# Two-layer recurrent and mixture-of-experts block on one core: recurrence pieces moved into the listing of rows, two weight loads moved among stores, row normalization moved to ScalarE

## The chip, the core and the metric

The program runs on one core of a Trainium2 chip. A core has a matrix engine (TensorE, PE in the profile; its weight loads are listed as PEld), three elementwise engines (VectorE as DVE, ScalarE as ACT, GpSimd as POOL) and a queue engine (SyncE as SP) that mostly issues DMAs. Every engine runs its own list of instructions in order and waits on semaphores where an operand isn't there yet; so an instruction that waits holds up all that is listed behind it on that engine. The metric is the time in microseconds of one execution of the whole program, as a median of runs.

## The reference

The input is one sequence of 2048 rows of 512 numbers. There are two layers; each computes `x + s * silu(f)`, where `s` is a mixer and `f` a mixture-of-experts network, both fed with the layer-normalized `x`. The change is in layer 0, cut here to what matters:

```python
xn = layernorm(x)
# mixer: token shift, three projections, a recurrence over time for each of 512 channels
xk, xv, xr = xn*tm + shifted(xn)*(1 - tm)          # three different tm
k, v, r = xk @ Wk.T, xv @ Wv.T, sigmoid(xr @ Wr.T)
for t in range(2048):                              # aa, bb, pp carried
    qt = max(pp, k[t] + u);  e1 = exp(pp - qt);  e2 = exp(k[t] + u - qt)
    wkv[t] = (e1*aa + e2*v[t]) / (e1*bb + e2)
    pn = max(pp - exp(w), k[t]);  f1 = exp(pp - pn);  f2 = exp(k[t] - pn)
    aa, bb, pp = f1*aa + f2*v[t], f1*bb + f2, pn
s = (r * layernorm(wkv, ln_g, ln_b)) @ Wo.T
# experts: each row goes to one of 2 by the larger gate logit
sel = argmax(xn @ gate_w.T)
f = top_w * ((silu(xn @ w_gate[sel].T) * (xn @ w_up[sel].T)) @ w_down[sel].T)
```

Layer 1 is an attention with pooled keys and a network of 16 routed and 2 shared experts; the change leaves its code alone.

## The kernel before

**First stage (L170 to L362).** Eight loads bring `x` to SBUF as `xin` (two tiles of 128 rows each, L177), and one brings Wk (L182). For each pair of tiles VectorE makes mean and variance (L129, L130), ScalarE normalizes in place (L234), and VectorE takes the difference of the two gate logits of each row (L238, into `dl`). Then each tile is turned by four PE transposes (L139), copied to `xt` by ScalarE (L140; three buffers) and stored by SP to a DRAM tensor `xnt0`, which holds the normalized rows turned (L245; 16 stores). Wv and Wr are loaded behind these stores (L248, L249). From `dl` VectorE then makes the listing: two small matmuls count the rows of each expert (L271), a chain of small VectorE operations (L277 to L337) gives every row a place in a list sorted by expert, VectorE makes one-hot tables (`put` L343, `hot` L350), and 16 matmuls (L355, 32 PE instructions[...]) turn these into the list `tok` of row numbers with `row_mr`, each listed row's mean and reciprocal deviation (L359, L360).

**Recurrence (L386 to L536).** `recurrence(b)` handles 256 time steps for all channels, eight blocks in all. It is a generator of 22 pieces, so that its work can be laid among other work piece by piece. In order: load the turned rows `xT` and take the difference `diff` to the row before (piece 1, POOL, L400); mix for k (2); mix for v and project half of k (3); mix for r and project the other half of k (4); two pieces with scans on k and the projections of v (5, 6); two with the projections of r and the differences under the exponentials (7, 8, L459 to L465); two sigmoids (9, L467, L468); two exponentials (10, L470, L471); scans `st_a` and `st_b` (L478), divisions, a normalization and the store. The carried states are columns 0 of `st_p`, `st_a`, `st_b`; block b starts with three ScalarE copies of the last column (L397). The projections share two PSUM buffers (`proj`), each free again when ScalarE has copied it out (L428, L430, L452, L467, L468).

**Layer 0's experts (L540 to L650).** The list is worked off in pairs of tiles. `rows0` gathers 128 rows per tile with an indirect DMA from POOL (`xr`, L545), normalizes them on VectorE with `row_mr` (L552), turns them with four PE transposes through one PSUM buffer (L560) and copies them to `xg` on ScalarE (L563). `up0` makes 16 PE instructions per unit (L571), a Silu on ScalarE (L576, `sg`) and a product on VectorE (L578, `hT`); `down0` (L593) runs two units later. Weights come in eight parts per pair through four buffers (`load0`, L157 and L161).

**What sets the order.** The program text gives each instruction a priority, and a scheduler at build time puts them in an order for each engine: what is ready earlier by its own estimate of times goes first, and among ready ones the text decides. Work can so be listed far ahead of its place in the text. `tc.keep_in_program_order(ins)` forbids this for one instruction: it stays behind all that the text has before it on its engine. Seven pieces of the recurrence stand in the text ahead of the experts (L692); from there on `pieces0` and the recurrence alternate, paced by `done * WORK < spent * PIECES * NRB` (L697).

Of the kernel before, what the change touches and what calls it, by code (L numbers as in the profile page):

```python
# [9 lines left out]
F32 = mybir.dt.float32  # L10
I32 = mybir.dt.int32
AF = mybir.ActivationFunctionType
ALU = mybir.AluOpType
# [4 lines left out]
P = 128  # L18
# [59 lines left out]
def tile_kernel(ctx: ExitStack, tc: tile.TileContext, a: dict):  # L78
# [89 lines left out]


# [55 lines left out]
    for i in range(0, NT, 2):  # L225
        xin = xins[i // 2]
        mv, rstd = norm_stats(xin, 2, all_mv[:, i : i + 2, :], facts[:, 2, i : i + 2])
        shift = small.tile([P, 2], F32, tag="shift", name="shift")
# [3 lines left out]
        for j in range(2):  # L232
            xn = xin[:, j, :]
            nc.scalar.activation(  # L234
                xn, xn, AF.Identity, bias=shift[:, j : j + 1], scale=rstd[:, j : j + 1],
            )
            junk = n0.tile([P, D], F32, tag="hot", bufs=2, name="junk")
            nc.vector.tensor_tensor_reduce(  # L238
                out=junk, in0=xn, in1=wdiff, scale=1.0, scalar=0.0, op0=ALU.mult, op1=ALU.add,
                accum_out=dl[:, i + j : i + j + 1],  # L240
            )
    for i in range(NT):
        xt = n0.tile([P, NC, P], F32, tag="xt", name="xt")
        transposed(n0ps, xins[i // 2][:, i % 2, :], xt, "tp")
        nc.sync.dma_start(out=xnt0[:, :, i * P : (i + 1) * P], in_=xt)  # L245
    wv = rc.tile([P, NC, D], F32, name="wv")
    wr = rc.tile([P, NC, D], F32, name="wr")
    tc.keep_in_program_order(nc.sync.dma_start(out=wv, in_=a["Wv"]))  # L248
    tc.keep_in_program_order(nc.sync.dma_start(out=wr, in_=a["Wr"]))  # L249
    nc.vector.tensor_copy(facts[:, 1, :], all_mv[:, :, 0])  # L250

    sel = n0.tile([P, NT, E0], F32, bufs=1, name="sel")
    nc.vector.tensor_scalar(
        out=sel[:, :, 0], in0=dl, scalar1=0.0, scalar2=None, op0=ALU.is_le
    )
    nc.vector.tensor_scalar(
# [83 lines left out]

    put = n0.tile([P, NT, 3, NST], F32, bufs=1, name="put")
# [6 lines left out]
    for i0 in range(0, NT, HN):  # L348
        hot = n0.tile([P, HN, P], F32, tag="hot", bufs=2, name="hot")
# [20 lines left out]
    zero = rc.tile([P, DX], F32, name="zero")  # L370
    nc.gpsimd.memset(zero, 0.0)
    S4 = [P, NC, RB]
    ones = rc.tile([P, P], F32, name="ones")
    nc.vector.memset(ones, 1.0 / D)
    nge = rc.tile([P, NC], F32, name="nge")
    nc.scalar.activation(nge, vecs[:, VEC.index("decay"), :], AF.Exp)
    nc.vector.tensor_scalar(out=nge, in0=nge, scalar1=-1.0, scalar2=None, op0=ALU.mult)

    st_p = rc.tile([P, NC, RB + 1], F32, name="st_p")
    st_a = rc.tile([P, NC, RB + 1], F32, name="st_a")  # L380
    st_b = rc.tile([P, NC, RB + 1], F32, name="st_b")
    nc.vector.memset(st_p[:, :, 0:1], -1.0e38)
    nc.vector.memset(st_a[:, :, 0:1], 0.0)
    nc.vector.memset(st_b[:, :, 0:1], 0.0)

    def recurrence(b):  # L386

        t0 = b * RB

        xT0 = rb.tile([P, NC, RB + 1], F32, tag="xT0", bufs=2, name="xT0")  # L390
        if b == 0:
            nc.vector.memset(xT0[:, :, 0:1], 0.0)
            nc.sync.dma_start(out=xT0[:, :, 1:], in_=xnt0[:, :, 0:RB])
        else:
            nc.sync.dma_start(out=xT0, in_=xnt0[:, :, t0 - 1 : t0 + RB])
            for st in (st_p, st_a, st_b):
                nc.scalar.copy(st[:, :, 0:1], st[:, :, RB : RB + 1])  # L397
        cur, prev = xT0[:, :, 1 : 1 + RB], xT0[:, :, 0:RB]
        diff = rb.tile(S4, F32, tag="diff", name="diff")
        nc.gpsimd.tensor_tensor(out=diff, in0=cur, in1=prev, op=ALU.subtract)  # L400
        yield

        def mixed(tm):
            xm = rb.tile(S4, F32, tag="xm", bufs=3, name="xm")
            for c in range(NC):
                nc.vector.scalar_tensor_tensor(
                    out=xm[:, c, :], in0=diff[:, c, :], scalar=vec(tm, c),
                    in1=prev[:, c, :], op0=ALU.mult, op1=ALU.add,
                )
            return xm  # L410

        def project(xm, w_, o0):
            ps = rps.tile([P, 2, RB], F32, tag="proj", name="proj")
            for j in range(2):
                for c in range(NC):
                    nc.tensor.matmul(  # L416
                        out=ps[:, j, :], lhsT=w_[:, c, (o0 + j) * P : (o0 + j + 1) * P],
                        rhs=xm[:, c, :], start=(c == 0), stop=(c == NC - 1),
                    )
            return ps  # L420

        k = rb.tile(S4, F32, tag="k", name="k")
        ku = rb.tile(S4, F32, tag="ku", name="ku")
        v = rb.tile(S4, F32, tag="v", name="v")
        r = rb.tile(S4, F32, tag="r", name="r")

        def take_k(o0, ps):
            nc.scalar.copy(k[:, o0 : o0 + 2, :], ps)  # L428
            for j in range(2):
                nc.scalar.activation(  # L430
                    ku[:, o0 + j, :], ps[:, j, :], AF.Identity, bias=vec("first", o0 + j)
                )

        def scan_p(c):
            nc.vector.tensor_tensor_scan(
                out=st_p[:, c, 1 : RB + 1],
                data0=nge[:, c : c + 1].to_broadcast([P, RB]),
                data1=k[:, c, :], initial=st_p[:, c, 0:1], op0=ALU.add, op1=ALU.max,
            )

        xk = mixed("tm_k")
        yield
        xv = mixed("tm_v")
        take_k(0, project(xk, wk, 0))
        yield
        xr = mixed("tm_r")
        take_k(2, project(xk, wk, 2))
        yield
        for o0 in (0, 2):
            scan_p(o0)  # L450
            scan_p(o0 + 1)
            nc.scalar.copy(v[:, o0 : o0 + 2, :], project(xv, wv, o0))  # L452
            yield
        pp, ppn = st_p[:, :, 0:RB], st_p[:, :, 1 : RB + 1]
        ex = rb.tile([P, 4, NC, RB], F32, tag="ex", name="ex")
        e1, e2, f1, f2 = (ex[:, i] for i in range(4))
        qt = rb.tile(S4, F32, tag="qt", name="qt")
        r01 = project(xr, wr, 0)
        nc.vector.tensor_tensor(out=f1, in0=pp, in1=ppn, op=ALU.subtract)  # L459
        nc.vector.tensor_tensor(out=f2, in0=k, in1=ppn, op=ALU.subtract)  # L460
        yield
        r23 = project(xr, wr, 2)
        nc.vector.tensor_tensor(out=qt, in0=pp, in1=ku, op=ALU.max)  # L463
        nc.gpsimd.tensor_tensor(out=e1, in0=pp, in1=qt, op=ALU.subtract)  # L464
        nc.gpsimd.tensor_tensor(out=e2, in0=ku, in1=qt, op=ALU.subtract)  # L465
        yield
        nc.scalar.activation(r[:, 0:2, :], r01, AF.Sigmoid)  # L467
        nc.scalar.activation(r[:, 2:4, :], r23, AF.Sigmoid)  # L468
        yield
        nc.scalar.activation(ex[:, 2:4], ex[:, 2:4], AF.Exp)  # L470
        nc.scalar.activation(ex[:, 0:2], ex[:, 0:2], AF.Exp)  # L471
        fv = qt
        nc.vector.tensor_tensor(out=fv, in0=f2, in1=v, op=ALU.mult)
        yield

        def scan(st, add, cs):
            for c in cs:
                nc.vector.tensor_tensor_scan(  # L478
                    out=st[:, c, 1 : RB + 1], data0=f1[:, c, :], data1=add[:, c, :],
                    initial=st[:, c, 0:1], op0=ALU.mult, op1=ALU.add,  # L480
                )

        scan(st_a, fv, (0, 1))
        nc.gpsimd.tensor_tensor(out=v, in0=e2, in1=v, op=ALU.mult)
        yield
        scan(st_a, fv, (2, 3))
        yield
        scan(st_b, f2, range(NC))
        yield
        num, den = ku, fv  # L490
        nc.vector.tensor_tensor(out=num, in0=e1, in1=st_a[:, :, 0:RB], op=ALU.mult)
        nc.gpsimd.tensor_tensor(out=den, in0=e1, in1=st_b[:, :, 0:RB], op=ALU.mult)
        yield
        nc.vector.tensor_tensor(out=num, in0=num, in1=v, op=ALU.add)
        nc.vector.tensor_tensor(out=den, in0=den, in1=e2, op=ALU.add)
        yield
        for c0 in (0, 2):
            for c in (c0, c0 + 1):
                nc.vector.reciprocal(out=den[:, c, :], in_=den[:, c, :])
            yield  # L500


        two = rb.tile([P, 2, RB], F32, tag="two", name="two")

        def mean(src):

            nc.vector.tensor_tensor(out=two, in0=src[:, 0:2], in1=src[:, 2:4], op=ALU.add)
            nc.vector.tensor_tensor(
                out=two[:, 0, :], in0=two[:, 0, :], in1=two[:, 1, :], op=ALU.add
            )  # L510
            pm = f0t.tile([P, 2, RB], F32, tag="tp", name="pm")[:, 0, :]
# [1374 lines left out]
```

## Time and profile before

| what | value |
|---|---|
| median of 3 runs | 1950.14 us (1944.71 to 1953.96) |
| the profiled execution | 1940.83 us |
| its span, first to last instruction | 1939.1 us |
| PE busy | 1857.2 us (96%) |
| PEld, DVE, ACT, POOL busy | 1292.1, 787.3, 532.9, 465.9 us |
| mean granted TensorE clock | 0.986 of full speed |
| DMA bytes, mean rate | 381.35 MB, 197 GB/s |
| first matmul of the experts (L571) | at 82.32 us |

Times within the span count from its first instruction. In a line of the timeline the columns are start, duration, engine, source line, operation, output and inputs, shape and count; brackets at the end give the engine's idle time before it and the instruction that ended it. In a table of stretches each engine has its busy time and count, then follow the granted TensorE clock (PEclk, 1.00 is full speed), the DMA engines' mean busy share and the rate in GB/s.

### The profile page before, as it was taken

How to read it: one execution, taken by the hardware profiler on the slowest of the kernel's cores; microseconds unless marked ns; L12 is line 12 of the kernel's file. 1: busy time of each engine (PE TensorE's matmuls, PEld its weight loads, DVE VectorE, ACT ScalarE, POOL GpSimd, SP SyncE). 2: the span in 40 equal slices, each digit the busy share in tenths (PEclk: the TensorE clock that was granted, in tenths of full speed). 3: DMA queues.
4: the chain of work that ended last, by engine and by line, in shares of the span. 5: the costliest groups of instructions: out<-in, count | busy, mean ns of one | idle time of the engine just before them, and what ended most of it. 6: DMA issues, size and time to landing. Idle time of an engine off the chain costs nothing.

```text
span 1939.1 us, 23212 instructions
## 1 busy us (share of the span) xinstructions
PE 1857.2 (96%) x8107; PEld 1292.1 (67%) x8107; DVE 787.3 (41%) x1565; ACT 532.9 (27%) x994; POOL 465.9 (24%) x350
## 2 busy tenths in 40 slices
PE   5899999999999999999989999999999999999977
PEld 4677777787877777777533654444767777777654
DVE  8713627272634545252166544331323232223116
ACT  6212322232323232232134212221222222222223
POOL 1301212121201111020210453000344444444430
PEclk9799999999999999999999999999999999999998
DMA  7548685635654443436461553022999999999963
GB/s 250 205 144 278 205 306 178 221 108 163 197 195 141 130 131 125 157 98 233 147 227 46 174 215 114 31 95 87 313 290 316 320 311 298 292 282 265 299 148 131
DMA packets 214096, 381.35 MB, mean 197 GB/s; under 512 B 16972, under 2 KB 134476, under 8 KB 213080
## 3 DMA queue, kind: packets, MB, share of 16 engines
q1 hardware_dynamic: 183896, 332.78, 50.7%
q0 software_dynamic: 28784, 45.63, 10.7%
q10 hardware_dynamic: 1296, 1.41, 0.3%
q8 instruction: 67, 1.10, 0.2%
q14 instruction: 53, 0.43, 0.1%
HBM read 294.04 MB, written 85.72 MB: 196 GB/s over the span
## 4 chain that ended last, share of the span: by engine, by line
PE 83%; DMA 6%; DVE 3%; issue 2%; POOL 2%; ACT 2%; SPq 0%; POOLq 0%; ACTq 0%; DVEq 0%
PE pg L571 23%; PE py L593 12%; PE ph L1685 9%; PE py L1709 9%; PE proj L416 7%; PE py L1105 4%; PE ph L956 3%; PE pw L1593 2%; DMA comb<-y,to 2%; PE pq L1352 2%; PE tp L1678 1%; PE po L712 1%; PE ps L1560 1%; PE pl L870 1%; PE pw L1477 1%
## 5 line engine op out<-in xcount | busy, mean ns | idle before, releaser
L571 PE MATMUL pg<-xg,w 128*128 128x256 f32 (+1 forms) x2304 | 497.8, 369 | 3.3 <-ACT xg L563 3.3
L571 PEld LDWEIGHTS pg<-xg,w 128*128 128x128 f32 x2304 | 420.9, 191 | 95.0 <-issue 42.1
L1717 POOL DMA_INDIRECT comb<-y,to x146 | 226.9, 1554 | 300.0 <-DMA comb<-y,to 222.2
L593 PE MATMUL py<-wd,hT 128*128 128x512 f32 x544 | 256.9, 593 | 2.9 <-DVE hT L578 2.9
L1685 PEld LDWEIGHTS ph<-xg,w 128*128 128x128 f32 (+1 forms) x1776 | 201.9, 182 | 39.8 <-ACT xg L1680 32.9
L1685 PE MATMUL ph<-xg,w 128*128 128x128 f32 (+1 forms) x1776 | 214.4, 277 | 1.5 <-DMA w<-in_w_dram 1.5
L1709 PE MATMUL py<-w,ht 128*128 128x512 f32 (+1 forms) x438 | 209.1, 593 | 0.0
L578 DVE TENSOR_TENSOR hT<-sg,pg 128x256 f32<-128x256 f32 (+1 forms) x144 | 57.0, 402 | 338.4 <-ACT sg L576 338.3
L576 ACT ACTIVATE sg<-pg 128x256 f32<-128x256 f32 (+1 forms) x144 | 53.5, 372 | 419.7 <-PE pg L571 419.4
L593 PEld LDWEIGHTS py<-wd,hT 128*128 128x128 f32 x544 | 102.1, 190 | 72.2 <-issue 61.9
L1714 DVE TENSOR_SCALAR y<-py,g 128x512 f32<-128x512 f32 x73 | 54.6, 749 | 206.7 <-PE py L1709 196.1
L942 ACT ACTIVATE ht<-ph,b1t 128x128 f32<-128x128 f32 (+1 forms) x222 | 81.3, 366 | 178.9 <-PE ph L1685 161.4
L1709 PEld LDWEIGHTS py<-w,ht 128*128 128x128 f32 (+1 forms) x438 | 75.1, 191 | 49.8 <-issue 49.3
L1680 ACT COPY xg<-tp 128x512 f32<-128x512 f32 x74 | 43.4, 586 | 177.2 <-PE tp L1678 166.4
L1105 PE MATMUL py<-w,hT 128*128 128x512 f32 (+1 forms) x192 | 89.3, 596 | 0.0
L956 PE MATMUL ph<-xT,w 128*128 128x512 f32 (+1 forms) x192 | 88.0, 597 | 0.0
L1043 POOL DMA_INDIRECT xs<-acc,slot x64 | 63.1, 985 | 67.2 <-DMA xs<-acc,slot 43.5
L1352 PE MATMUL pq<-xT,wqg 128*128 128x256 f32 x224 | 56.6, 401 | 14.2 <-DVE wide L1572 9.6
L712 PE MATMUL po<-wo,yb 128*128 128x512 f32 x128 | 59.3, 620 | 9.6 <-ACT acc L721 5.5
L416 PE MATMUL proj<-xm,wr 128*128 128x256 f32 x256 | 60.9, 393 | 5.6 <-ACT v L452 5.6
L464 POOL TENSOR_TENSOR ex<-st_p,qt 128x1024 f32<-128x1024 f32 x8 | 18.3, 2288 | 193.0 <-DVE qt L463 193.0
L1678 PEld LDWEIGHTS tp<-ident,x 128*128 128x128 f32 x296 | 36.7, 140 | 38.8 <-issue 21.5
(418 smaller groups left out, 2180.9 us busy)
## 6 DMA issues: line engine op xcount, KB each, us to landing
w<-in_w_dram SPq DMA_DIRECT2D x76, 704.0 KB
w<-in_w_dram SPq DMA_DIRECT2D x76, 512.0 KB
w<-in_w_gate_dram SPq DMA_DIRECT2D x72, 512.0 KB
w<-in_w_up_dram SPq DMA_DIRECT2D x72, 512.0 KB
wd<-in_w_down_dram SPq DMA_DIRECT2D x72, 512.0 KB
xs<-zero SPq DMA_DIRECT2D x16, 1360.0 KB
x<-xs SPq DMA_DIRECT2D x74, 272.0 KB
w<-in_w_dram SPq DMA_DIRECT2D x76, 192.0 KB
```

What stands on the lines that cost most here:

```text
L416: nc.tensor.matmul(out=ps[:, j, :], lhsT=w_[:, c, (o0 + j) * P : (o0 + j + 1) * P], rhs=xm[:, c, :], start=(c == 0), stop=(c == NC - 1),)
L571: nc.tensor.matmul(out=pg[:, i, 0:n], lhsT=w[:, c, i * FH + f * P : i * FH + (f + 1) * P], rhs=xg[:, c, 0:n], start=(c == 0), stop=(c == N ...
L593: nc.tensor.matmul(out=p, lhsT=hT[:, u * P : (u + 1) * P], rhs=wd[:, f, :], start=first_, stop=last_,)
L712: nc.tensor.matmul(out=po, lhsT=yb[:, c, s * P : (s + 1) * P], rhs=wo[:, c, :], start=(c == 0), stop=(c == NC - 1),)
L942: nc.scalar.activation(dst, src, AF.Relu, bias=b)
L956: nc.tensor.matmul(out=ph[0:n, :], lhsT=up(w, f, n, c), rhs=xT[:, c, cols], start=(c == 0), stop=(c == NC - 1),)
L1043: ins = nc.gpsimd.indirect_dma_start(out=xs, out_offset=bass.IndirectOffsetOnAxis(ap=slot[:, i, k : k + 1], axis=0), in_=acc[:, i, :], in_ ...
L1105: nc.tensor.matmul(out=py, lhsT=hT[0:n, e, f, s * P : (s + 1) * P], rhs=down(w, f, n), start=(e == 0 and f == 0), stop=(e == NS - 1 and f ...
L1352: nc.tensor.matmul(out=pq[:, j, :], lhsT=w[:, c, w0 : w0 + P], rhs=xT[:, c, tc0], start=(c == 0), stop=(c == NC - 1),)
L1685: nc.tensor.matmul(out=ph[0:n, :], lhsT=up(w, f, n, c), rhs=xg[:, c, :], start=(c == 0), stop=(c == NC - 1),)
L1709: nc.tensor.matmul(out=py, lhsT=hT[0:n, f, :], rhs=down(w, f, n), start=(f == 0), stop=(f == NF1 - 1),)
L1717: nc.gpsimd.indirect_dma_start(out=c_, out_offset=bass.IndirectOffsetOnAxis(ap=to, axis=0), in_=y[:, h * D // 2 : (h + 1) * D // 2], in_of ...
```

## The change

1. The whole text from the constants `zero`, `ones`, `nge` and the states to the end of `recurrence` moves from behind the listing to the head of the first stage. This lets pieces be drawn earlier: two ahead of `sel`, one ahead of `put`, one between the second and third `hot` table. So `done` starts at 4, and two more pieces stand ahead of the experts: six in all instead of seven.
2. Pins: the first instruction of the listing (`sel`) stays behind the two pieces on VectorE; block 0's two exponentials stay behind all earlier ScalarE text, its sigmoids included; block 1's three state copies stay behind all earlier ScalarE text, that of the experts included.
3. `diff` of blocks 0 and 1 is made on VectorE instead of POOL.
4. Wv is loaded behind the fifth store of a turned tile, Wr behind the ninth, instead of both behind the sixteenth.
5. Gathered rows are normalized on ScalarE as scale times row plus bias. The bias is minus mean times reciprocal deviation, which was made anyway for L234; it now goes straight into the table `facts`, and the copy of the means (L250) falls away.

```diff
@@ ahead of the first stage: zero .. recurrence, moved here; changed lines of it alone @@
             for st in (st_p, st_a, st_b):
-                nc.scalar.copy(st[:, :, 0:1], st[:, :, RB : RB + 1])
+                ins = nc.scalar.copy(st[:, :, 0:1], st[:, :, RB : RB + 1])
+                if b == 1:
+                    tc.keep_in_program_order(ins)
...
-        nc.gpsimd.tensor_tensor(out=diff, in0=cur, in1=prev, op=ALU.subtract)
+        (nc.vector if b < 2 else nc.gpsimd).tensor_tensor(
+            out=diff, in0=cur, in1=prev, op=ALU.subtract
+        )
...
-        nc.scalar.activation(ex[:, 2:4], ex[:, 2:4], AF.Exp)
-        nc.scalar.activation(ex[:, 0:2], ex[:, 0:2], AF.Exp)
+        ins = nc.scalar.activation(ex[:, 2:4], ex[:, 2:4], AF.Exp)
+        if b == 0:
+            tc.keep_in_program_order(ins)
+        ins = nc.scalar.activation(ex[:, 0:2], ex[:, 0:2], AF.Exp)
+        if b == 0:
+            tc.keep_in_program_order(ins)
@@ first stage @@
-        shift = small.tile([P, 2], F32, tag="shift", name="shift")
+        shift = facts[:, 1, i : i + 2]
...
+    wv = rc.tile([P, NC, D], F32, name="wv")
+    wr = rc.tile([P, NC, D], F32, name="wr")
     for i in range(NT):
...
         nc.sync.dma_start(out=xnt0[:, :, i * P : (i + 1) * P], in_=xt)
-    wv = rc.tile([P, NC, D], F32, name="wv")
-    wr = rc.tile([P, NC, D], F32, name="wr")
-    tc.keep_in_program_order(nc.sync.dma_start(out=wv, in_=a["Wv"]))
-    tc.keep_in_program_order(nc.sync.dma_start(out=wr, in_=a["Wr"]))
-    nc.vector.tensor_copy(facts[:, 1, :], all_mv[:, :, 0])
-
+        for at, w_, nm in ((4, wv, "Wv"), (8, wr, "Wr")):
+            if i == at:
+                tc.keep_in_program_order(nc.sync.dma_start(out=w_, in_=a[nm]))
+
+    blocks = (piece for b in range(NRB) for piece in recurrence(b))
+    for _ in range(2):
+        next(blocks)
     sel = n0.tile([P, NT, E0], F32, bufs=1, name="sel")
-    nc.vector.tensor_scalar(
+    ins = nc.vector.tensor_scalar(
         out=sel[:, :, 0], in0=dl, scalar1=0.0, scalar2=None, op0=ALU.is_le
     )
+    tc.keep_in_program_order(ins)
...
+    next(blocks)
     put = n0.tile([P, NT, 3, NST], F32, bufs=1, name="put")
...
     for i0 in range(0, NT, HN):
+        if i0 == 2 * HN:
+            next(blocks)
         hot = n0.tile([P, HN, P], F32, tag="hot", bufs=2, name="hot")
@@ rows0 @@
-            nc.vector.tensor_scalar(
-                out=xr, in0=xr, scalar1=row_mr[:, 0, j : j + 1],
-                scalar2=row_mr[:, 1, j : j + 1], op0=ALU.subtract, op1=ALU.mult,
+            nc.scalar.activation(
+                xr, xr, AF.Identity, bias=row_mr[:, 0, j : j + 1], scale=row_mr[:, 1, j : j + 1]
             )
@@ the main loop @@
-    blocks = (piece for b in range(NRB) for piece in recurrence(b))
-    done = 0
+    done = 4
...
-    for _ in range(7):
+    for _ in range(6 - done):
```

## The prediction

> **What bounds the kernel now.** I read the page's engine shares first: PE is busy for 1857.2 of 1939.1 us, so only PE's idle time (82 us) and its time at a lower clock can be won. The table of stretches says where these lie: from 100 to 480 us PE is never idle, the rest of the idle time is mostly the change of layers at 940 to 1100 us and the end from 1850 us, which the change leaves alone. The first 100 us are what it touches:
>
> ```profile
> 30.00:40.00 10.00, 10.00 (x53) 8.39 (x52) 8.11 (x26) 6.53 (x12) 1.97 (x1) 1.00 0.70 207
> 40.00:50.00 10.00, 4.58 (x25) 4.08 (x23) 8.28 (x30) 3.07 (x7) 0.37 (x1) 0.85 0.94 306
> 50.00:60.00 10.00, 10.00 (x41) 9.06 (x41) 5.72 (x9) 1.91 (x1) 3.80 (x3) 0.63 1.02 373
> 60.00:70.00 10.00, 4.45 (x18) 3.50 (x17) 7.26 (x8) 4.17 (x5) 5.65 (x4) 0.88 1.07 371
> 70.00:80.00 10.00, 8.99 (x36) 7.22 (x34) 9.53 (x13) 1.46 (x4) 4.44 (x2) 0.78 0.12 44
> ```
>
> Columns: PE, PEld, DVE, ACT, POOL busy, then clock, DMA share, GB/s. PE loses 5.42 us in 40 to 50 and 5.55 us in 60 to 70, the clock is below full from 46 us to about 90, and the DMA engines are saturated from 40 to 70. The timeline names the gaps (last bracket of a line):
>
> ```profile
> 47.36 7.07 PE L355 MATMUL tab<-put,hot 128*128 128x51 f32 x32 [5.42 <-DVE put L343]
> 54.23 8.67 PE L416 MATMUL proj<-xm,wv 128*128 128x256 f32 x32
> 68.45 6.64 PE L416 MATMUL proj<-xm,wr 128*128 128x256 f32 x16 [5.55 <-ACT v L452]
> 82.32 13.44 PE L571 MATMUL pg<-xg,w 128*128 128x256 f32 x48 [3.33 <-ACT xg L563]
> 97.31 3.62 PE L571 MATMUL pg<-xg,w 128*128 128x256 f32 x16
> ```
>
> The second and third gap both end with ScalarE, so I read its own list, and VectorE's row normalizations beside it:
>
> ```profile
> 57.04 1.91 ACT L470 ACTIVATE ex<-ex 128x2048 f32<-128x2048 f32 x1 [12.56 <-DVE ex L460]
> 63.72 0.20 ACT L397 COPY st_p<-st_p 128x4 f32<-128x4 f32 x1 [4.76 <-POOL ex L464]
> 66.01 1.91 ACT L471 ACTIVATE ex<-ex 128x2048 f32<-128x2048 f32 x1 [2.09 <-POOL ex L465]
> 67.83 1.05 ACT L452 COPY v<-proj 128x512 f32<-128x512 f32 x2
> 79.56 0.20 ACT L397 COPY st_a<-st_a 128x4 f32<-128x4 f32 x1 [3.36 <-DVE ku L491]
> 81.59 0.20 ACT L397 COPY st_b<-st_b 128x4 f32<-128x4 f32 x1 [1.83 <-POOL qt L492]
> 81.69 0.58 ACT L563 COPY xg<-tp 128x512 f32<-128x512 f32 x1
> 62.74 4.44 DVE L552 TENSOR_SCALAR xr<-xr,row_mr 128x512 f32<-128x512 f32 x3 [4.59 <-issue]
> ```
>
> The `v` copies need only PE's projection, done at 62.9, but are listed behind block 1's `st_p` copy and block 0's second exponential, which wait for POOL's L464 and L465, and these sit behind four gathers. PE waits for a `proj` buffer meanwhile. The last `xg` copy (transposes done at about 78.2) stands behind the `st_a` and `st_b` copies in the same way. So the gaps are an order of listing on ScalarE, not a lack of work.
>
> **The pins.** Block 1's copies and block 0's exponentials are just the four instructions in front of those two. Behind the pins they can't stand there: the exponentials come after the sigmoids, the copies after the first Silus. What that returns: the gap of 5.55, the gap of 3.33, and clock. The `wr` run above took 6.64 us for 16 against 3.62 for 16 at 97 us, so 3.0 lost; the experts' first 48 took 13.44 against three times 3.45 (16 instructions' pitch in the chain of waits), so 3.1 lost. Here a rule weighs in: the Trainium skill, TensorE: Matmul & The Clock Gate, section "What's actually happening", lets PE fall to half clock after an idle window of some 3.4 us and recover after about 3.4 us of work; by it each gap costs half of 3.4, 1.7 us, and the two returns would be 3.4 in place of 6.1. The trace has clock 0.50 for about 6 us after each of these gaps, so I take 6.1. Price of the pins: VectorE's scans L478 wait for later exponentials, and behind them in its list stand the experts' products L578. Estimate 0 to 5 us, once; I take 0, since `down0` runs two units (two times 5.17 us) behind.
>
> **PE's new sequence.** The listing's matmuls end at 54.43 now. Then `wv` 8.67, still cold; `wr` 32 instructions at full pitch 6.9; two sets of transposes at 0.60; then the experts, at 54.4 + 8.7 + 6.9 + 1.2 = 71.2 if nothing is late. Gathered rows must be there: the first landed at 62.74 (VectorE stood ready from 58.2), and then come two normalizations at 0.80, two transposes at 0.60, two copies at 0.58, some 4 us: 66.7. That lies ahead of 71.2, so PE's own work decides. If `wr` is left behind the start, the start is 66.7 and 6.9 us of work come later: equal to 73.6. Drawing six pieces instead of seven therefore costs at most 2.4 us; I take 0.
>
> **Wv and Wr.** Each is 1024 KB; at 373 GB/s (row of 50 to 60) both take 5.6 us. Now they are issued at 44.35 and 45.02, and expert weights queue behind. After, they go at about 24 and 31, ahead of 11 and 7 stores. Gain: the saturated stretch that the gathers run in ends up to 5.6 us earlier; I count 0, since PE decides. With Wv there, `wv` projections could also fill PE's gap of 5.42 us, which would give up to that and its 1.8 us of cold loss (8.67 against 6.9); whether they are listed there nothing in this trace tells. From 0 to 7.2; I take 0. Loss: SP's issue of 0.62 and 0.44 is small, but the stores queue in the DMA engines behind 1 MB each. A store already takes 3.5 us and more (the load of `xT` waits 2.0 us for one), and there are three `xt` buffers, so ScalarE's copy of tile i+3 waits for the store of tile i: the trace has the copy at 27.03 some 0.1 us behind the landing of the fourth store. A delayed copy holds ScalarE, behind it the normalizations L234, then L238 and `sel`. From 0 to 5.6; I take 2, as two normalizations already stand between such copies.
>
> **`diff` and the copy of the means.** POOL's `diff` takes 1.89 us (L400); VectorE has 1.22 for the same shape (L459), so twice 1.22 are added to VectorE. Taken away are the copy L250 (1.81 us) and the stretching of L288:
>
> ```profile
> 26.34 1.81 DVE L250 COPY facts<-all_mv 128x16 f32<-128x16 f32 x1
> 38.03 2.33 POOL L400 TENSOR_TENSOR diff<-xT 128x1024 f32<-128x1024 f32 x1 [9.92 <-DVE run L279]
> 38.59 1.79 DVE L288 TENSOR_TENSOR full<-run,eno 128x8 f32<-128x8 f32 x1
> ```
>
> L288 handles 8 elements; its neighbours of that size take 0.15, so 1.64 us of it is the POOL instruction beside it. Net 1.81 + 1.64 - 2.44 = 1.0 us earlier on the path from `dl` to `tok`, all on VectorE, which is busy there. With the 2 us of the stores the listing is 1 us later: start 72.2.
>
> **Rows on ScalarE.** 0.80 us (L234, same shape, scale and bias from SBUF) against 0.546 at the median on VectorE: 17 times 0.26 = 4.4 us more. The skill's page ScalarE: Activation LUTs, "Rules for kernel authors", speaks against it: multiplications and additions belong on VectorE. By that rule alone the edit costs up to 4.4 us; the rows say it is hidden, as ScalarE is 27% busy and a Silu comes once per 5.17 us; and three of these on VectorE took 4.44 us beside POOL's L464 and L465, one of them 3.53. I take 0. What moves with it is the wait: VectorE stood 43.4 us in ten waits for gathers, the longest 8.2, with the products L578 behind; after, ScalarE stands, with the Silus and the `proj` copies behind. PE has two units less the Silu and product, some 9.2 us, before it notices.
>
> **Sum.** 82.3 - 72.2 = 10.1, which holds both gaps, the `wr` clock and the listing's 1 us; plus 3.1 for the experts' warm start: 13.2 us. On the profiled execution that is 1940.8 to 1927.6. That execution lies 9.3 us below the median of the runs shown, so I take the difference to the median: 1950.1 - 13.2 = 1937. A measurement of this kernel tells about 0.5% (10 us) from no change.
>
> **Rivals.** *The order stays short of it* (chance 0.20): other instructions come to stand before the `v` and `xg` copies, or the stores' 5.6 us fall fully on the listing. For it: the order is found at build time, by estimates that missed the gathers here by 4.6 us. Against it: the four instructions that blocked are pinned. It gives 13.2 less about 8: 1945.
>
> *ScalarE is held by the gathers* (0.20), the slower side: eight pairs of rows are gathered behind the first. If one holds ScalarE for more than 9.2 us, PE stops for the rest. For it: in-order queueing, and table loads of 1.28 us join the wait. Against it: the longest wait seen is 8.2 us, with two small PE stops in the whole stage. At 12.5 us per pair PE loses 3.3 times 8 = 26 us: 1937 + 26 = 1963. It decides from 23 us, that is 12 us per pair.
>
> *The loads do all of it* is a reading rather than a time: if `wv` fills the first gap, 1937 - 7 = 1930, within the forecast's own range.
>
> **Numbers.** Forecast 0.60, its own range 1928 to 1945; of it 0.57 are faster by over 0.5%, 0.03 within. The first rival gives 0.04 faster, 0.14 same, 0.02 slower; the second 0.01 same, 0.19 slower. Together 0.61, 0.18, 0.21. The range reaches from 1926 (0.05 below: all open terms at their good ends) to 1960 (0.14 above).
>
> **What would show it.** The idle before the `wr` projections and before the first L571 near zero; first L571 at 70 to 73; clock 1.00 from there; the gap before L355 as now. A wait of ScalarE's L552 successor above 9 us with PE idle would show the second rival; ScalarE waiting for `xnt0` stores at 28 to 40 us the first. The forecast is wrong if PE's total idle time isn't some 8 us less.

## The result and the profile after

The kernel after takes 1938.23 us at the median of 16 runs (1929.68 to 1942.98), the kernel before in the same session 1945.25 us (16 runs, 1938.61 to 1957.56). The ratio of the runs is 0.9953 with a 95% interval of 0.9936 to 0.9969, so the change is worth 9.1 us (6.0 to 12.4); the quotient of the two medians alone would be 0.9964. The forecast was 1937 us, 13.2 us less than the 1950.14 us of the three runs that it started from. The profiled execution has a span of 1936.9 us; PE is busy for 1854.5 us of it (before 1857.2 of 1939.1), at a mean clock of 0.987. The two profiled executions differ by 2.2 us of span only: the kernel after leads by 12.4 us at the end of layer 0 and loses most of that later. The measured times, not these two spans, say what the change is worth.

The table of stretches of the kernel after, with the columns as before:

```profile
30.00:40.00 10.00, 9.81 (x52) 8.10 (x51) 8.01 (x29) 6.59 (x11) 0.00 (x0) 1.00 0.93 262
40.00:50.00 10.00, 8.34 (x42) 6.92 (x41) 9.96 (x22) 4.16 (x8) 2.12 (x1) 1.00 0.89 275
50.00:60.00 10.00, 7.01 (x32) 6.05 (x30) 8.24 (x15) 1.87 (x2) 2.55 (x2) 0.79 1.01 321
60.00:70.00 10.00, 8.66 (x35) 7.46 (x33) 0.67 (x3) 0.72 (x2) 4.05 (x4) 0.70 1.03 353
70.00:80.00 10.00, 9.26 (x47) 8.06 (x48) 1.67 (x4) 7.01 (x10) 3.85 (x3) 1.00 0.44 137
```

PE is now busy for 43.1 of these 50 us (38.0 before), and the clock is full in 70 to 80, where it was 0.78. PE's timeline in the kernel after shows which gaps went:

```profile
45.48 4.91 PE L219 MATMUL proj<-xm,wv 128*128 128x256 f32 x22
50.23 1.89 PE L219 MATMUL proj<-xm,wr 128*128 128x256 f32 x8
55.12 3.09 PE L538 MATMUL tab<-put,hot 128*128 128x51 f32 x16 [2.99 <-DVE put L524]
58.00 2.04 PE L219 MATMUL proj<-xm,wr 128*128 128x256 f32 x4
59.83 3.49 PE L538 MATMUL tab<-put,hot 128*128 128x51 f32 x16
63.12 5.54 PE L219 MATMUL proj<-xm,wr 128*128 128x256 f32 x18
70.74 0.66 PE L574 MATMUL tp<-ident,xr 128*128 128x128 f32 x4 [2.08 <-ACT xr L567]
73.86 10.52 PE L585 MATMUL pg<-xg,w 128*128 128x256 f32 x48
85.94 3.62 PE L585 MATMUL pg<-xg,w 128*128 128x256 f32 x16
```

The gaps ahead of the `wr` projections (5.55 us) and of the first expert matmul (3.33 us) are gone. That matmul comes at 73.86 us (before 82.32) and its first 48 take 10.52 us (before 13.44). But the road there isn't the one foretold: all of `wv` and 12 of the 32 `wr` instructions lie ahead of or among the listing's matmuls (L538), and these end at 63.3 us, where they ended at 54.4. VectorE's timeline in the kernel after tells why the list is late, POOL's beside it:

```profile
39.47 1.22 DVE L201 TENSOR_TENSOR diff<-xT 128x1024 f32<-128x1024 f32 x1
43.78 1.22 DVE L262 TENSOR_TENSOR ex<-st_p 128x1024 f32<-128x1024 f32 x1
45.02 1.22 DVE L263 TENSOR_TENSOR ex<-k,st_p 128x1024 f32<-128x1024 f32 x1
46.58 1.22 DVE L266 TENSOR_TENSOR qt<-st_p,ku 128x1024 f32<-128x1024 f32 x1
48.06 2.28 DVE L209 SCALAR_TENSOR_TENSOR xm<-diff,vecs,xT 128x256 f32<-128x256 f32 x1
50.26 2.32 DVE L512 TENSOR_SCALAR at<-at 128x16 f32<-128x16 f32 x1
53.33 0.68 DVE L533 TENSOR_TENSOR hot<-place,col 128x512 f32<-128x512 f32 x1
63.36 0.18 DVE L542 CAST tok<-tab 128x17 int32<-128x17 f32 x1 [3.64 <-PE tab L538]
...
47.88 2.17 POOL L267 TENSOR_TENSOR ex<-st_p,qt 128x1024 f32<-128x1024 f32 x1 [44.59 <-DVE qt L266]
50.02 2.53 POOL L268 TENSOR_TENSOR ex<-ku,qt 128x1024 f32<-128x1024 f32 x1
64.58 1.20 POOL L560 DMA_INDIRECT xr<-in_x_dram,tok  x1 [12.04 <-DMA w<-in_w_gate_dram]
```

Block 1's `diff` and block 0's differences `f1`, `f2` and `qt` (L262, L263, L266) now stand inside the listing: four times 1.22 us. `qt` sets free POOL's two subtractions, and beside them a mix (L209, elsewhere 0.48) takes 2.28 us and L512, on 16 elements a partition, 2.32. Together 4.9 + 1.8 + 2.2 = 8.9 us. `tok` comes at 63.36 us instead of 54.47, also 8.9 us later, and the first gather with it at 64.6 instead of 55.6. That the two figures are equal is chance: `sel` comes 1.5 us earlier than before and L288's successor (L468) is 1.7 us shorter, while two more scans (L238), more mixes and four `wr` instructions among the listing's matmuls take about as much.

### The profile page after: what moved, and what is told of

Same layout as the page of the kernel before. It is cut to its first block, busy times and chain, and to the rows that moved or that the text cites. A ratio compares the mean times of both kernels' runs of the same rounds, so it can differ in the third digit from the quotient of the medians.

```text
span 1936.9 us, 23219 instructions
## 1 busy us (share of the span) xinstructions
PE 1854.5 (96%) x8107; PEld 1288.4 (67%) x8107; DVE 774.8 (40%) x1549; ACT 544.4 (28%) x1011; POOL 460.2 (24%) x348
## 3 DMA queue, kind: packets, MB, share of 16 engines
q10 hardware_dynamic: 1296, 1.41, 0.3%
## 4 chain that ended last, share of the span: by engine, by line
PE 55%; DMA 7%; ACT 1%; issue 1%; DVE 1%; POOL 1%; SPq 0%; ACTq 0%; POOLq 0%; DVEq 0%
PE ph L1698 9%; PE py L1722 9%; PE pg L585 8%; PE py L607 4%; PE py L1118 4%; DMA comb<-y,to 3%; PE ph L969 3%; PE proj L219 2%; PE pw L1606 2%; PE pq L1365 2%; PE tp L1691 1%; PE po L725 1%; PE ps L1573 1%; PE pl L883 1%; PE pw L1490 1%
## 5 line engine op out<-in xcount | busy, mean ns | idle before, releaser
L1365 PE MATMUL pq<-xT,wqg 128*128 128x256 f32 x224 | 56.1, 398 | 18.7 <-DVE wide L1585 13.8
L1365 PEld LDWEIGHTS pq<-xT,wqg 128*128 128x128 f32 x224 | 43.4, 202 | 26.2 <-DVE wide L1585 14.2
```

What stands on the lines that cost most here:

```text
L1365: nc.tensor.matmul(out=pq[:, j, :], lhsT=w[:, c, w0 : w0 + P], rhs=xT[:, c, tc0], start=(c == 0), stop=(c == NC - 1),)
```

## The experiments

Two accounts of the gain were to be told apart. The prediction's: the pins take ScalarE's two stalls away and the early loads give nothing. The rival: the early loads let `wv` and part of `wr` run where PE had been idle ahead of the list, and that alone does it. Further open: what put the recurrence into the listing, whether that costs anything, and whether ScalarE's waits for gathers do.

All gains in one table, each from 11 or 12 runs (16 for the kernel after) against the kernel before on the same chip. "Layer 0 ends" is the start of the last expert matmul of layer 0 (`down0`) in the profiled execution.

| kernel | first gather, us | first expert matmul, us | layer 0 ends, us | ratio, 95% interval | gain, us |
|---|---|---|---|---|---|
| before | 55.6 | 82.3 | 951.5 | | |
| before, profiled again | 53.9 | 80.7 | 948.7 | | |
| after | 64.6 | 73.9 | 939.1 | 0.9953 (0.9936 to 0.9969) | 9.1 |
| pins only | 55.3 | 70.0 | 937.2 | 0.9945 (0.9928 to 0.9963) | 10.7 |
| after without pins | 65.2 | 75.9 | 939.8 | 0.9959 (0.9941 to 0.9977) | 8.0 |
| after, loads late | 61.0 | 74.5 | 947.0 | 1.0002 (0.9983 to 1.0021) | -0.4 |
| after, listing first | 52.9 | 66.9 | 934.8 | 0.9929 (0.9905 to 0.9953) | 13.8 |
| loads only | 58.7 | 75.6 | 939.7 | 0.9942 (0.9919 to 0.9965) | 11.3 |
| loads and pins | 56.5 | 71.5 | 938.6 | 0.9954 (0.9934 to 0.9975) | 8.9 |
| after, rows on VectorE | 64.8 | 72.7 | 938.2 | 0.9962 (0.9940 to 0.9984) | 7.4 |
| after, pieces drawn late | 63.5 | 75.6 | 941.0 | 0.9950 (0.9924 to 0.9977) | 9.7 |
| after, `diff` on GpSimd | 54.8 | 69.4 | 935.6 | 0.9951 (0.9928 to 0.9973) | 9.5 |

**Pins only.** To the kernel before:

```diff
-                nc.scalar.copy(st[:, :, 0:1], st[:, :, RB : RB + 1])
+                ins = nc.scalar.copy(st[:, :, 0:1], st[:, :, RB : RB + 1])
+                if b == 1:
+                    tc.keep_in_program_order(ins)
...
-        nc.scalar.activation(ex[:, 2:4], ex[:, 2:4], AF.Exp)
-        nc.scalar.activation(ex[:, 0:2], ex[:, 0:2], AF.Exp)
+        ins = nc.scalar.activation(ex[:, 2:4], ex[:, 2:4], AF.Exp)
+        if b == 0:
+            tc.keep_in_program_order(ins)
+        ins = nc.scalar.activation(ex[:, 0:2], ex[:, 0:2], AF.Exp)
+        if b == 0:
+            tc.keep_in_program_order(ins)
```

> The kernel before with one edit: block 0's two exponentials and block 1's three state copies stay behind all earlier ScalarE text. Theory (the four instructions on ScalarE made the second and third gap of PE): both gaps close, the first L571 comes at 70 to 72 us instead of 82.3, and the time is that of before less 10 to 14 us (ratio 0.993 to 0.995), as much as the whole change. Rival (the gain is that Wv comes early and fills the first gap): ratio 0.998 to 1.001, first L571 after 78 us.

PE's timeline of this kernel is the one that the prediction drew for the change:

```profile
47.02 7.07 PE L355 MATMUL tab<-put,hot 128*128 128x51 f32 x32 [5.41 <-DVE put L343]
53.88 8.71 PE L418 MATMUL proj<-xm,wv 128*128 128x256 f32 x32
62.44 3.62 PE L418 MATMUL proj<-xm,wr 128*128 128x256 f32 x16
69.96 10.60 PE L577 MATMUL pg<-xg,w 128*128 128x256 f32 x48
```

The first gap stays, the other two are gone, and the start at 69.96 lies within 1.3 us of the prediction's 71.2. So the reading of ScalarE's order was right, and the pins alone bring 10.7 us (7.2 to 14.0), as the theory expected.

**After without pins.** The same diff, backwards, in the kernel after; the pin of `sel` stays.

> The changed kernel without the pins of block 0's exponentials and block 1's state copies; the pin of the listing's first instruction stays. Theory (the pins carry the gain): the row copies wait behind the state copies again, first expert matmul at 78 to 84 us instead of 73.9, 5 to 9 us above the changed kernel. Rival (the early Wv and the moved text have already taken the projections of v and r out of the way, so there is nothing left to hold up): within 2 us of the changed kernel.

8.0 us (4.5 to 11.5) are left, and the start comes at 75.9 us, not at 78 to 84: the rival's expectation is met. In the kernel after the pins are therefore worth nothing that can be measured. ScalarE's timeline of this kernel shows that they do act on the order:

```profile
51.83 0.20 ACT L196 COPY st_p<-st_p 128x4 f32<-128x4 f32 x1 [0.71 <-POOL ex L265]
54.31 1.91 ACT L272 ACTIVATE ex<-ex 128x2048 f32<-128x2048 f32 x1 [2.29 <-POOL ex L266]
56.13 0.57 ACT L253 COPY v<-proj 128x512 f32<-128x512 f32 x1
```

The exponential and the `st_p` copy stand ahead of the second `v` copy again, as before. But POOL's subtractions now lie ahead of the gathers, so they hold that copy only until 56.1 us. In this kernel PE first waits 3.71 us for `put` and begins the listing's matmuls at 57.1: nothing is lost there.

**After, loads late.** Wv and Wr go behind the sixteenth store again:

```diff
-        for at, w_, nm in ((4, wv, "Wv"), (8, wr, "Wr")):
-            if i == at:
-                tc.keep_in_program_order(nc.sync.dma_start(out=w_, in_=a[nm]))
+    tc.keep_in_program_order(nc.sync.dma_start(out=wv, in_=a["Wv"]))
+    tc.keep_in_program_order(nc.sync.dma_start(out=wr, in_=a["Wr"]))
```

> The changed kernel with Wv and Wr loaded behind the sixteenth store again. Theory of the prediction (the loads count 0, PE's own work decides): within 2 us of the changed kernel. Rival, seen in the trace (v's projections now run inside the listing, which the early load allows): PE is idle 5 us more in the listing, and stores no longer hold up ScalarE, 3 to 6 us above the changed kernel at the first expert matmul counted with the projections that are still open.

The gain is gone whole: 1.0002, an interval that does not meet that of the kernel after. That is 9.5 us worse, more than the 3 to 6 us of the rival. PE's and ScalarE's timelines of this kernel:

```profile
51.05 1.19 PE L219 MATMUL proj<-xm,wv 128*128 128x256 f32 x2 [9.84 <-DMA wv<-in_Wv_dram]
59.59 9.02 PE L219 MATMUL proj<-xm,wv 128*128 128x256 f32 x28
...
72.00 0.56 ACT L255 COPY v<-proj 128x512 f32<-128x512 f32 x1
```

The scheduler puts two `wv` instructions ahead of the listing's matmuls, and PE stands 9.84 us for Wv. Most of this it would have stood for `put` anyway, which VectorE finishes at 48.8 us; Wv costs the listing some 3 us more. The second `v` copy ends behind four row normalizations, so 24 of the 32 `wr` instructions and eight of block 1's `wk`, which the kernel after has done by then, are left for after the start of the experts. That is about 7 us of PE: from the first expert matmul to the end of layer 0 this kernel takes 872.5 us, the kernel after 865.2. So a start at 74.5 us is worth little here. Given the rest of the change, the early loads are what carries it. The pins are still in this kernel and alone they had brought 10.7 us; which of the other edits takes that away, no run here shows.

**Loads only.** The kernel before with Wv issued behind the fifth store and Wr behind the ninth, and nothing else:

```diff
+    wv = rc.tile([P, NC, D], F32, name="wv")
+    wr = rc.tile([P, NC, D], F32, name="wr")
     for i in range(NT):
...
+        for at, w_, nm in ((4, wv, "Wv"), (8, wr, "Wr")):
+            if i == at:
+                tc.keep_in_program_order(nc.sync.dma_start(out=w_, in_=a[nm]))
-    wv = rc.tile([P, NC, D], F32, name="wv")
-    wr = rc.tile([P, NC, D], F32, name="wr")
-    tc.keep_in_program_order(nc.sync.dma_start(out=wv, in_=a["Wv"]))
-    tc.keep_in_program_order(nc.sync.dma_start(out=wr, in_=a["Wr"]))
```

> The kernel before with Wv and Wr issued among the stores and nothing else. Theory 1 (two ways to one gain): with Wv in SBUF by about 36 us the block's Wv projections stand among the listing's matmuls, the gap of 5.4 us before them shrinks to under 2 us, both exponentials stay in front of the second xg copy on ScalarE and may hold it, and the first expert matmul comes at 68 to 76 us (before 82.3): ratio 0.993 to 0.997. Theory 2 (the prediction's: the loads are worth 0 by themselves, the pins are the gain): the first expert matmul stays at 79 us or later, since ScalarE's order still holds v or xg, and the ratio is 0.998 to 1.002.

Theory 1 holds: 11.3 us (6.8 to 15.8) without a pin. PE's timeline of this kernel:

```profile
40.12 2.75 PE L417 MATMUL proj<-xm,wv 128*128 128x256 f32 x12
48.10 2.60 PE L356 MATMUL tab<-put,hot 128*128 128x51 f32 x16 [1.41 <-DVE put L344]
59.16 6.36 PE L417 MATMUL proj<-xm,wr 128*128 128x256 f32 x20
68.73 0.63 PE L561 MATMUL tp<-ident,xr 128*128 128x128 f32 x4 [3.22 <-POOL ex L466]
75.64 10.52 PE L572 MATMUL pg<-xg,w 128*128 128x256 f32 x48
```

`wv` fills what was a gap of 5.42 us. The second `v` copy comes at 59.4 us and waits for PE's projection alone. The second exponential does stand ahead of the second `xg` copy (73.2 us), and eight of block 1's `wk` instructions ahead of the experts, so the start is not early; yet the work done by then is worth it.

**Loads and pins.** Both of these edits in the kernel before.

> The kernel before with Wv and Wr issued among the stores and ScalarE's exponentials and state copies pinned, but the recurrence where it was (no pieces in the listing, diff on GpSimd, rows on VectorE). If the two gains add, the first expert matmul comes at 62 to 65 us and the ratio is 0.989 to 0.992. If they are one gain (PE then stands at the first gathered rows, ready 10 to 12 us after the list), it comes at 66 to 70 us and the ratio is 0.992 to 0.995, as with the pins alone (0.9945).

They do not add: 8.9 us (4.9 to 12.8), a start at 71.5, both slightly worse than expected even of one gain alone. PE's timeline of this kernel shows where the second gain went:

```profile
56.06 4.48 PE L419 MATMUL proj<-xm,wr 128*128 128x256 f32 x20
66.54 1.09 PE L567 MATMUL tp<-ident,xr 128*128 128x128 f32 x4 [5.99 <-POOL ex L468]
...
63.27 3.16 DVE L559 TENSOR_SCALAR xr<-xr,row_mr 128x512 f32<-128x512 f32 x1 [4.55 <-issue]
```

PE has done its projections by 60.5 us and stands for 5.99 us. What it waits for are the first gathered rows: they were gathered from 56.5 us on, and their normalization on VectorE begins at 63.27. It takes 3.16 us, where the median is 0.55, beside the POOL subtractions L467 and L468, the second of which the profile therefore names. So about half of the wait is for the rows and half for this one instruction; with the loads only it takes 3.35 us, which spans nearly all of the 3.22 us gap there. On ScalarE the same work took 0.81 us beside the same subtractions (after, `diff` on GpSimd). Each edit fills PE up to the first rows; the second fills nothing more.

**After, pieces drawn late.** All six pieces are drawn behind the listing, as in the kernel before:

```diff
-    for _ in range(2):
-        next(blocks)
...
-    next(blocks)
     put = n0.tile([P, NT, 3, NST], F32, bufs=1, name="put")
...
-        if i0 == 2 * HN:
-            next(blocks)
...
-    done = 4
+    done = 0
...
-    for _ in range(6 - done):
+    for _ in range(6):
```

> The kernel after with no piece of the recurrence drawn ahead of or inside the listing: all six are drawn behind it, as before; the rest as in the kernel after. If the draws put the recurrence's VectorE work into the listing, the first gather comes at 54 to 58 us (kernel after 64.6, kernel before 55.6) and the first expert matmul at 66 to 70 us. If the order on VectorE doesn't follow the draws but what is ready by the estimates, f1, f2, qt and block 1's diff stay in the listing, the first gather stays at 61 to 66 us and the first expert matmul at 71 to 76 us: ratio 0.994 to 0.998, as the kernel after.

The second account holds. The first gather stays late, at 63.5 us, `f1`, `f2` and `qt` stay in the listing, and the ratio is 0.9950. Where the text draws the pieces, the part of the change that gave it its name, makes no difference that can be seen.

**After, `diff` on GpSimd.**

```diff
-        (nc.vector if b < 2 else nc.gpsimd).tensor_tensor(
-            out=diff, in0=cur, in1=prev, op=ALU.subtract
-        )
+        nc.gpsimd.tensor_tensor(out=diff, in0=cur, in1=prev, op=ALU.subtract)
```

> The kernel after with diff of all blocks on GpSimd, as before. By the prediction the move of diff to VectorE is worth about -0.8 us on the listing (2.44 added, 1.64 of stretching taken away), so without it the list comes 0 to 1 us earlier or later than the kernel after's: first gather at 64 to 65.5 us. If the move is what lets block 0's f1, f2 and qt run ahead of the list, they stand behind hot without it: first gather at 54 to 58 us, first expert matmul at 66 to 70 us, last matmul of the first layer's experts at 934 to 937 us, ratio 0.991 to 0.994.

VectorE's timeline of this kernel:

```profile
37.90 1.80 DVE L442 TENSOR_SCALAR topw<-topw 128x16 f32<-128x16 f32 x1
45.42 0.14 DVE L510 TENSOR_SCALAR at<-at 128x16 f32<-128x16 f32 x1
46.31 0.68 DVE L531 TENSOR_TENSOR hot<-place,col 128x512 f32<-128x512 f32 x1
48.57 1.22 DVE L260 TENSOR_TENSOR ex<-st_p 128x1024 f32<-128x1024 f32 x1
53.64 0.18 DVE L540 CAST tok<-tab 128x17 int32<-128x17 f32 x1 [1.52 <-PE tab L536]
```

It was the move of `diff` that let block 0 run ahead of the list; by what estimates the scheduler did so is not on record. Without it `f1` comes behind the second `hot`, and `tok` at 53.64, 9.7 us earlier. The experts start 4.5 us and layer 0 ends 3.5 us earlier than in the kernel after. The expected ratio below 0.994 did not come: 0.9951, with an interval of 4.4 us to either side. So the profile shows the move to cost some 4 us of start, and the measured times neither confirm nor exclude it.

**After, listing first.** The kernel after with four VectorE instructions pinned behind the listing's:

```diff
-        (nc.vector if b < 2 else nc.gpsimd).tensor_tensor(
+        ins = (nc.vector if b < 2 else nc.gpsimd).tensor_tensor(
             out=diff, in0=cur, in1=prev, op=ALU.subtract
         )
+        if b == 1:
+            tc.keep_in_program_order(ins)
...
-        nc.vector.tensor_tensor(out=f1, in0=pp, in1=ppn, op=ALU.subtract)
-        nc.vector.tensor_tensor(out=f2, in0=k, in1=ppn, op=ALU.subtract)
+        for o_, i_ in ((f1, pp), (f2, k)):
+            ins = nc.vector.tensor_tensor(out=o_, in0=i_, in1=ppn, op=ALU.subtract)
+            if b == 0:
+                tc.keep_in_program_order(ins)
...
-        nc.vector.tensor_tensor(out=qt, in0=pp, in1=ku, op=ALU.max)
+        ins = nc.vector.tensor_tensor(out=qt, in0=pp, in1=ku, op=ALU.max)
+        if b == 0:
+            tc.keep_in_program_order(ins)
```

> The changed kernel with four more pins on VectorE: block 0's two differences under the exponentials and its maximum, and block 1's first difference, stay behind the listing. Theory (the list of rows came 9 us later, 63.3 instead of 54.4 us, because the recurrence's VectorE and POOL work was listed among the listing): the list is ready at 52 to 55 us, the first expert matmul at 64 to 68 us instead of 73.9, 5 to 9 us below the changed kernel. Rival (the list isn't what the experts wait for; PE has projections to do until 73 anyway, or the scans that are moved behind stop the experts later): within 2 us of the changed kernel.

It has the earliest list (first gather 52.9), the earliest start (66.9) and the best ratio, 0.9929. Its interval meets that of the kernel after at 0.9936 to 0.9953, so it is the best candidate, not a shown improvement on it; the 4.7 us between the two gains also fall just short of the 5 to 9 expected.

**After, rows on VectorE.**

```diff
-            nc.scalar.activation(
-                xr, xr, AF.Identity, bias=row_mr[:, 0, j : j + 1], scale=row_mr[:, 1, j : j + 1]
-            )
+            nc.vector.tensor_scalar(
+                out=xr, in0=xr, scalar1=row_mr[:, 1, j : j + 1],
+                scalar2=row_mr[:, 0, j : j + 1], op0=ALU.mult, op1=ALU.add,
+            )
```

> The kernel after with the gathered rows normalized on VectorE as before. If ScalarE's in-order wait for gathers costs nothing (the prediction), ratio to the kernel before 0.994 to 0.997, as the kernel after has it (0.9953). If that wait costs PE time over the 17 row tiles, this kernel is 2 to 8 us faster than the kernel after: 0.991 to 0.994. If VectorE's wait is the dearer one, since the experts' products stand behind it, it is 2 to 8 us slower: 0.997 to 1.000.

0.9962, which can't be told from 0.9953. From the first expert matmul to the end of layer 0 both profiles have the same time: 865.5 us here, 865.2 in the kernel after. The wait only changes engines. The chain of waits (total us, times, longest), in the kernel after and then, in a fence of its own, here:

```profile
ACT xr L567 <- DMA xr<-in_x_dram,tok: 53.0, 14, 9.1
```

```profile
DVE xr L567 <- DMA xr<-in_x_dram,tok: 52.9, 14, 8.2
```

**The kernel before, again.** Unchanged.

> The kernel before, unchanged, profiled a second time. If the times in the first stage repeat, the first expert matmul is at 82 +- 1 us and the last matmul of the first layer's experts starts at 951.5 +- 1.5 us. If the lead of 12 us that the kernel after has there over one profile is partly that profile's own, it starts 2 us or more earlier. The second layer's expert stage takes 500 to 514 us in the six profiles so far whatever the kernel; if that is run to run, it is not 500.6 us again.

Its first expert matmul comes at 80.7 us and layer 0 ends at 948.7, 1.7 and 2.8 us earlier than in the profile that the prediction worked from. Against the mean of the two, 950.1, the kernel after leads by 11.0 us at that point, not by 12.4, and the ten changed kernels by 11.0 on average; their mean measured gain is 8.8. Where the other 2.2 us go stays open. From there on nothing systematic can be read from single profiles: from the end of layer 0 to the last instruction the two profiles of the kernel before take 987.6 and 994.8 us and the changed ones 991.4 to 1008.3; the experts of layer 1 alone, from their first to their last second product, take 500.6 and 506.4 us and 500.6 to 513.7.

## Why the prediction came near in size and was half right in cause

**The two stalls on ScalarE: right.** Both gaps are gone in the kernel after, and the pins alone remove them. **The pins as the cause of the gain in this change: wrong.** In the kernel before either the pins or the loads suffice. In the kernel after the pins can go (8.0 us left) and the loads can't (-0.4 us). The forecast came near because it counted one of two ways to the same gain.

**"I count 0, since PE decides" and "I take 0" for Wv and Wr: the step that failed.** The upper bound, 0 to 7.2, had the mechanism in it, and the third rival named it. What was missed is that with `wv` and part of `wr` done ahead of the list PE has less left behind it, so that the list may come late. In the loads' own run this gave 11.3 us; taking them out of the change took all of its 9.1. The loss of 2 us by delayed stores did not reach the listing: ScalarE waits 5.6 us in six times for stores, but `sel` comes at 32.80 us, earlier than before (34.31). What waits are the last transposes, with a PE gap of 1.64 us.

**"Net 1.81 + 1.64 - 2.44 = 1.0 us earlier": wrong by some ten.** L250's copy is gone (the 1.5 us at `sel`) and L288 is no longer stretched. But the sum took the order on VectorE as given. With `diff` ready earlier, 8.9 us of other work came into the listing, and the stretching only moved from L288 to L512.

**"So PE's own work decides": wrong for this change.** It holds in the pins-only kernel, where PE has no gap ahead of the experts. In the kernel after PE waits for the rows: gather at 64.58, ScalarE's normalization from 69.87, PE's gap of 2.08 us ended by it. Where the loads are early and the list comes earlier than here, the wait is longer: 3.22 us with the loads only, 3.39 with the listing first, 4.06 with `diff` on GpSimd, 5.99 with loads and pins.

**The sum.** The start was to move from 82.3 to 72.2 and came at 73.9: 8.5 us in place of 10.1. The warm start was to give 3.1 and gave 13.44 - 10.52 = 2.9. So 13.2 became 11.4 by the profile that the prediction worked from. By the second profile of the kernel before, the start moves by 6.8 us and the first 48 matmuls by 12.31 - 10.52 = 1.8, together 8.6, beside a measured 9.1. The 13.2 us forecast lie above the measured interval of 6.0 to 12.4.

Luck has two parts in how near it came. The list was to be ready at 55.4 us with 16.8 us of PE's work behind it, and came at 63.3 with 10.5 behind it: misses of 7.9 and 6.3 us that nearly cancel. And 1937 us was counted from a median of three runs that lies 4.9 us above that of the sixteen.

**"The forecast is wrong if PE's total idle time isn't some 8 us less": it isn't less in the two profiles.** It is 81.9 us before and 82.4 after (86.5 in the second profile of before). In the first 100 us, where the change acts, it falls by 7.6 us, from 31.6 to 24.0; the profile of the kernel after has as much more idle time later. The two profiles of the kernel before alone differ by 4.6 us in this sum, so one pair of profiles can't decide it. Of the other signs that the prediction names, the start came at 73.9 us and not at 70 to 73, and the gap ahead of the listing's matmuls is 2.99 us and not 5.42 as before; the clock is at 1.00 from the start on, as foretold.

**Clock: one profile was too little to set against the rule.** The rule cited from the Trainium skill (TensorE: Matmul & The Clock Gate, "What's actually happening") gave 1.7 us for a gap; the prediction took the 3.0 and 3.1 us of its trace. In the second profile of the kernel before, the same two gaps cost 6.04 - 3.62 = 2.4 us and 12.31 - 10.52 = 1.8 us:

```profile
66.77 6.04 PE L416 MATMUL proj<-xm,wr 128*128 128x256 f32 x16 [4.46 <-ACT v L452]
80.65 12.31 PE L571 MATMUL pg<-xg,w 128*128 128x256 f32 x48 [3.94 <-ACT xg L563]
```

Nor is the clock below full all the way from 46 to 90 us in the kernel before, as the prediction reads the rows of 10 us: in rows of 2 us it is 1.00 from 58 to 66 and from 76 to 80. And the kernel after keeps a cold stretch at the listing's matmuls, behind its gap of 2.99 us, although PE is busy in all of it:

```profile
53.00:55.00 2.00, 0.00 (x0) 0.00 (x0) 2.00 (x7) 0.00 (x0) 0.00 (x0) 1.00 0.99 335
55.00:57.00 2.00, 1.89 (x12) 1.89 (x12) 1.53 (x4) 0.00 (x0) 0.00 (x0) 0.69 1.10 402
57.00:59.00 2.00, 2.00 (x9) 1.82 (x9) 0.99 (x3) 0.00 (x0) 0.00 (x0) 0.50 1.04 358
...
63.00:65.00 2.00, 2.00 (x7) 1.64 (x7) 0.67 (x3) 0.00 (x0) 0.42 (x1) 0.50 1.11 363
65.00:67.00 2.00, 2.00 (x9) 1.69 (x8) 0.00 (x0) 0.60 (x1) 1.70 (x2) 0.75 1.04 374
```

That is about 10 us at half clock, as behind the gap of 5.41 us in the pins-only kernel; with the loads only it is 13 us behind a gap of 1.41, and with `diff` on GpSimd, behind a gap of 0.72, the clock stays at 1.00. Here the measurements differ from the rule, by which an idle window of some 3.4 us comes first and about 3.4 us of work ends the cold stretch. What sets its length, no run here shows.

**Rows on ScalarE, 0: right** to within the interval. ScalarE's longest wait for gathered rows, 9.1 us, stayed just below the 9.2 us beyond which the slower rival had PE stop, and PE was busy for 379.7 of the 380 us from 100 to 480. **Six pieces in place of seven, 0:** not tried; the kernel with pieces drawn late draws six as well.

## What to carry to other kernels

When two edits both fill idle time ahead of the same event, find what that event waits for next (here the first gathered rows): together they earn only up to there, and the second is worth next to nothing beside the first. Which of the two can then be dropped depends on the rest of the kernel: here the pins could and the loads could not. Where a scheduler orders the work, an edit that makes an operand ready earlier must be costed with the order it brings about; moving two subtractions to another engine let 8.9 us of foreign work and of waiting beside it into the critical listing. And before a lead of a few us in one trace is set against a median, profile the unchanged kernel a second time.

## What the runs showed of the hardware

A VectorE instruction's time can depend wholly on POOL: the same `at` operation on 128x16 took 2.32 us beside POOL's subtraction L268 and 0.14 us without it, and `topw` on 128x16 took 1.80 us beside POOL's `diff` and 0.17 in the kernel with pieces drawn late, which makes that `diff` on VectorE. In these cases the price is about one POOL instruction (1.9 to 2.5 us), however small the VectorE one is. It is not always VectorE that pays: in the kernel before, POOL's L492 took 3.46 us beside VectorE's L491, which kept its 1.21 us; the same POOL operation took 2.18 us in the kernel after without pins, beside a VectorE one that took 3.87. With loads late, the 1 MB load of Wv that had been issued at 43.5 us, with the DMA engines' busy share at 1.01, let PE begin only at 51.05: some 7.6 us, where 1 MB alone at the stretch's 356 GB/s would take an estimated 2.9.
